# A four-layer graph network on one core: relational values with nodes on partitions, and attention terms spread over partitions by DMA through DRAM

## The chip, the cores and the metric

The kernel runs on one core of a Trainium2 chip. Times are device microseconds (us), the median of several executions. All executions told of here are in the same, fast state. The engines are named as in the profile: PE is TensorE (PEld its weight loads), DVE is VectorE, ACT is ScalarE, POOL is GpSimd, SP is SyncE, which issues most DMAs.

## The reference, cut to what matters

128 graphs of 64 nodes with 256 features each go through four layers, each with a layernorm ahead of it and a residual addition behind it:

```python
h = relu(layernorm(x)); x = x + gat4(h, adj)        # layer 0: attention, 4 heads
h = relu(layernorm(x)); x = x + gat1(h, adj)        # layer 1: attention, 1 head
h = relu(layernorm(x)); x = x + relational(h, adj)  # layer 2
h = relu(layernorm(x)); x = x + ggnn(h, adj)        # layer 3: 3 rounds of A h, then a GRU cell

# attention: e[i,j] = leaky_relu(e_src[i] + e_dst[j], 0.2), softmax over neighbours j,
#            out = elu(softmax @ Wh)
# relational, the part that these 0/1 edges use:
#            v = (h W.T + b) * sigmoid(h W.T Wg.T + bg);  out = relu((adj == 1).T @ v)
```

Everything is float32. The kernel factors the exponential of the leaky ReLU: up to a factor that the softmax cancels, it is max(exp(e_dst), exp(0.2 e_dst) * exp(-0.8 e_src)). The last factor, here called the spread term, belongs to node i, and for the product it must stand along the free axis, the same on all 64 partitions of the graph.

## The kernel before

16 groups of 8 graphs go through a pipeline of four stages, so a steady step has layer 0 of one group, layer 1 of the group before it, the relational layer of the third and the recurrence of the fourth. Their instructions are emitted side by side and ordered by the compiler. The parts that matter:

```python
# attention (both layers): the spread term, by a product with a matrix of ones per graph
nc.gpsimd.tensor_tensor(dg..., diag..., es[:, :, :heads]..., ALU.mult)       # e_src on a diagonal
for c in range(0, gh, step):
    nc.tensor.matmul(pe[:, : n * N], same, dg[:, c : c + n, :]..., ...)
    nc.scalar.activation(t[:, c : c + n, :]..., pe[:, : n * N], AF.Exp, scale=ALPHA - 1.0)
nc.vector.tensor_tensor(t, t, flat(gd), ALU.mult)
nc.vector.tensor_tensor(t, t, flat(fd), ALU.max)
for half in range(2):
    nc.vector.tensor_tensor(eb[b, :, b]..., t[b]..., mt[b]..., ALU.min)      # mask
# ... eb is the stationary operand of the aggregation

def elu_add(work, src, o):                       # end of both attention layers
    nc.vector.tensor_scalar(em, o, 0.0, None, op0=ALU.min)
    nc.scalar.activation(em, em, AF.Exp)
    nc.vector.scalar_tensor_tensor(em, em, -1.0, o, op0=ALU.add, op1=ALU.max)
    nc.gpsimd.tensor_tensor(src, src, em, ALU.add)      # the residual addition, xg<-xg,em

# relational layer: features on partitions, then eight transposes back
for c in range(K):
    for part in range(2):
        for k in range(K):
            nc.tensor.matmul(pm, wl[:, k, col : col + P], hT[:, k, :], ...)
    nc.scalar.activation(sg, pgh[1], AF.Tanh, bias=bl[:, 1, c : c + 1], scale=0.5)
    nc.scalar.activation(vT[:, c, :], pgh[0], AF.Identity, bias=bl[:, 0, c : c + 1])
    nc.vector.scalar_tensor_tensor(vT[:, c, :], sg, 1.0, vT[:, c, :], op0=ALU.add, op1=ALU.mult)
# ... then 4 x 2 nc.tensor.transpose(pt..., vT..., ident), and nc.scalar.copy(v..., pt)

def along(psum, hnat, abd, aT, c):               # recurrence: neighbours' sum
    # four products into pa
    nc.vector.tensor_copy(aT[:, c, :], pa)       # aT feeds the next gate products
```

The waits of TensorE are named below by what it waits for. "hn" is the layernorm's output, which is transposed. "hT" of the recurrence is the new state, which is transposed back (VectorE's last instruction of an update). "aT" is the copied neighbours' sum. "eb" is the masked attention terms, and "hnat" the copy of the recurrence's state with nodes on partitions. VectorE writes all.

Of the kernel before, what the change touches and what calls it, by code (L numbers as in the profile page):

```python
# [8 lines left out]
F32 = mybir.dt.float32  # L9
I32 = mybir.dt.int32  # L10
AF = mybir.ActivationFunctionType
ALU = mybir.AluOpType
# [3 lines left out]
P = 128  # L16
N = 64
D = 256
K = D // P
G = 4  # L20
T = G * P
# [3 lines left out]
ALPHA = 0.2  # L25
# [13 lines left out]
def over_partitions(ap, n):  # L39

    return bass.AP(tensor=ap.tensor, offset=ap.offset, ap=[[0, P], [1, n]])
# [25 lines left out]
def kernel(  # L67
# [28 lines left out]
    nc = tc.nc  # L96
# [14 lines left out]
    ident = const.tile([P, P], F32, name="ident")  # L111
    mhalf = const.tile([P, G], F32, name="mhalf")

    same = const.tile([P, P], F32, name="same")
    diag = const.tile([P, N], F32, name="diag")
# [246 lines left out]
    with ExitStack() as s1:  # L362
        once = s1.enter_context(tc.tile_pool(name="once", bufs=1))
        work = s1.enter_context(tc.tile_pool(name="work", bufs=2))
        psum = s1.enter_context(tc.tile_pool(name="psum", bufs=2, space=PSUM))

        class Layer:


# [7 lines left out]
                    return work.tile(shape, dtype, name=name, tag=name, bufs=self.shared[name])  # L377
                return self.pool.tile(shape, dtype, name=f"{name}{self.layer}", bufs=self.bufs.get(name, 1))

        W = [Layer(0, work, {"wh": 2, "es": 2, "fd": 2, "gd": 2}), Layer(1, work, {}), Layer(2, work, {"sg": 2})]  # L380

        nc.scalar.dma_start(w0e[:, :, :D], rows(W0))
        AT, XG, AG = [], [], []
# [20 lines left out]
        for s in range(2):  # L404
            h = slice(s * N, (s + 1) * N)
# [27 lines left out]
        OH = blocks("oh", G)  # L433
        ABD = blocks("abd", G)
        wl = once.tile([P, K, 2 * D], F32, name="wl")
        bl = once.tile([P, 2, K], F32, name="bl")

        def edge_bounds(g):

# [16 lines left out]
        def attention(g, layer, heads, we, mt):  # L456


            pool = W[layer]
            gh = G * heads  # L460
            src = XG[g]
            wv, es = yield from values(pool, psum, src, heads, we)
            fd = pool.tile([P, G, heads], F32, name="fd")
            gd = pool.tile([P, G, heads], F32, name="gd")
            nc.scalar.activation(fd, es[:, :, heads:], AF.Exp)
            nc.scalar.activation(gd, es[:, :, heads:], AF.Exp, scale=ALPHA)
            dg = pool.tile([P, gh, N], F32, name="dg")
            nc.gpsimd.tensor_tensor(
                dg.rearrange("p (g h) i -> p g h i", g=G),
                diag[:, None, None, :].to_broadcast([P, G, heads, N]),  # L470
                es[:, :, :heads, None].to_broadcast([P, G, heads, N]),
                ALU.mult,
            )
            yield 0.3
            t = pool.tile([P, gh, N], F32, name="t")
            step = 512 // N
            for c in range(0, gh, step):
                n = min(step, gh - c)
                pe = psum.tile([P, 512], F32, name="mm")
                nc.tensor.matmul(  # L480
                    pe[:, : n * N], same, dg[:, c : c + n, :].rearrange("p c i -> p (c i)"), start=True, stop=True
                )
                nc.scalar.activation(
                    t[:, c : c + n, :].rearrange("p c i -> p (c i)"), pe[:, : n * N], AF.Exp, scale=ALPHA - 1.0
                )
                yield 0.86
            flat = lambda d: d.rearrange("p g h -> p (g h)")[:, :, None].to_broadcast([P, gh, N])
            nc.vector.tensor_tensor(t, t, flat(gd), ALU.mult)  # L488
            nc.vector.tensor_tensor(t, t, flat(fd), ALU.max)  # L489
            eb = EB[layer][g % len(EB[layer])]  # L490
            for half in range(2):
                b = slice(half * N, (half + 1) * N)
                nc.vector.tensor_tensor(  # L493
                    eb[b, :, b].rearrange("p (g h) i -> p g h i", g=G),
                    t[b].rearrange("p (g h) i -> p g h i", g=G),
                    mt[b, :, None, :].to_broadcast([N, G, heads, N]),
                    ALU.min,
                )
            yield 0.3
            o = yield from aggregate(pool, psum, lambda p, h: eb[:, p * heads + h, :], wv, heads)  # L500
            elu_add(pool, src, o)

        def later_weights(prep):
            relational_weights(prep, psum, wl, W_loop, Wg_loop, 0.5)
            ihn = prep.tile([P, 6, D], F32, name="ihn")
            nc.scalar.dma_start(ihn, rows(w_ih))
            ihT = prep.tile([P, K, 3 * D], F32, name="ihT")
            transpose_blocks(psum, ihT, ihn, 6)
            hhn = prep.tile([P, 6, D], F32, name="ihn")
            nc.scalar.dma_start(hhn, rows(w_hh))  # L510
            transpose_blocks(psum, whh[:, :, : 2 * D], hhn[:, :4], 4)
            transpose_blocks(psum, whh[:, :, 2 * D :], hhn[:, 4:], 2, 0.5)
            for i in range(LAYERS):
                wn = prep.tile([P, K, D], F32, name="wn")
                nc.scalar.dma_start(wn, rows(weight[i]))
                wT = prep.tile([P, K, D], F32, name="gT")
                transpose_blocks(psum, wT, wn, K)

                for f in range(K):
                    for c0, c1 in ((0, 512), (512, 3 * D)):  # L520
                        pm = psum.tile([P, 512], F32, name="mm")
                        for k in range(K):
                            nc.tensor.matmul(
                                pm[:, : c1 - c0], wT[:, k, f * P : (f + 1) * P], ihT[:, k, c0:c1],
                                start=(k == 0), stop=(k == K - 1),
                            )
                        nc.vector.tensor_copy(wc[:, i, f, c0:c1], pm[:, : c1 - c0])
            with nc.allow_non_contiguous_dma(reason="biases onto partitions"):
                nc.scalar.dma_start(bl[:, 0, :], b_loop.rearrange("o (c p) -> p (o c)", p=P))
                nc.scalar.dma_start(bl[:, 1, :], bg_loop.rearrange("o (c p) -> p (o c)", p=P))  # L530
                nc.scalar.dma_start(bi, b_ih.rearrange("(c p) -> p c", p=P))
                nc.scalar.dma_start(bh, b_hh.rearrange("(c p) -> p c", p=P))
            nc.vector.tensor_scalar(bl, bl, 0.5, None, op0=ALU.mult)
            nc.vector.tensor_tensor(brz, bi[:, :4], bh[:, :4], ALU.add)
            nc.vector.tensor_scalar(brz, brz, 0.5, None, op0=ALU.mult)
            nc.vector.tensor_scalar(bh[:, 4:], bh[:, 4:], 0.5, None, op0=ALU.mult)

        def loop_relation(g):

            pool = W[2]  # L540
            src = XG[g]
            hT = pool.tile([P, K, T], F32, name="hT")
            yield from layernorm_T(pool, psum, src, hT)
            oh = OH[g % 2]
            block_diagonal(oh, AG[g], 1.0, ALU.is_equal)

            vT = pool.tile([P, K, T], F32, name="vT")
            for c in range(K):
                pgh = []
                for part in range(2):  # L550
                    pm = psum.tile([P, T], F32, name="mm")
                    col = part * D + c * P
                    for k in range(K):
                        nc.tensor.matmul(pm, wl[:, k, col : col + P], hT[:, k, :], start=(k == 0), stop=(k == K - 1))  # L554
                    pgh.append(pm)
                    yield 1.72
                sg = pool.tile([P, T], F32, name="sg")
                nc.scalar.activation(sg, pgh[1], AF.Tanh, bias=bl[:, 1, c : c + 1], scale=0.5)
                nc.scalar.activation(vT[:, c, :], pgh[0], AF.Identity, bias=bl[:, 0, c : c + 1])
                nc.vector.scalar_tensor_tensor(vT[:, c, :], sg, 1.0, vT[:, c, :], op0=ALU.add, op1=ALU.mult)  # L560
            v = pool.tile([P, G, D], F32, name="v")
            for q in range(G // 2):
                pt = psum.tile([P, 2, D], F32, name="tp")
                po = psum.tile([P, 2, D], F32, name="mm")
                ps = slice(2 * q, 2 * q + 2)
                for i in range(2):
                    p = 2 * q + i
                    for c in range(K):
                        nc.tensor.transpose(pt[:, i, c * P : (c + 1) * P], vT[:, c, p * P : (p + 1) * P], ident)
                nc.scalar.copy(v[:, ps, :], pt)  # L570
                yield 0.45
                for i in range(2):
                    p = 2 * q + i
                    nc.tensor.matmul(po[:, i, :], oh[:, p, :], v[:, p, :], start=True, stop=True)
                nc.vector.scalar_tensor_tensor(src[:, ps, :], po, 0.0, src[:, ps, :], op0=ALU.max, op1=ALU.add)
                yield 0.86
# [267 lines left out]
```

## Time and profile before

| what | before |
|---|---|
| time, median of 3 runs | 1795.34 us (1793.3 to 1802.8) |
| TensorE busy | 92% |
| VectorE busy | 55% |
| a steady step | 103.4 to 105.9 us |
| TensorE's waits at a step's end | 1.2 us (hT) and 3.3 us (hn) |

The prediction shows the busy shares, the chain, the steps and the step's end. One more view: VectorE in the middle of a step, in time (start, duration, engine, line, operation, output and inputs, shapes, and in brackets its idle time before with what ended it):

```profile
870.92 1.90 DVE L488 TENSOR_TENSOR t<-t,gd 128x1024 f32<-128x1024 f32 x1 [1.48 <-ACT t L483]
872.86 1.22 DVE L489 TENSOR_TENSOR t<-t,fd 128x1024 f32<-128x1024 f32 x1
874.60 0.68 DVE L246 COPY aT<-tp 128x512 f32<-128x512 f32 x1
875.20 2.44 DVE L493 TENSOR_TENSOR eb<-t,mt 64x1024 f32<-64x1024 f32 x2
```

The spread terms t start a block in which VectorE has no idle time, and the copy of aT stands within that block. So its place in the block decides when TensorE gets it.

### The profile page before, as it was taken

To read this page: it belongs to the slowest core of one execution; us is meant where nothing else is said; L and a number is where in the kernel's file an instruction comes from. 1 tells how busy PE (TensorE), PEld (TensorE's weight loads), DVE (VectorE), ACT (ScalarE), POOL (GpSimd) and SP (SyncE) were. 2 spreads that over 40 slices of the span, in tenths; PEclk is the share of its full clock that TensorE was granted. 3 is DMA by queue.
4 is the path that set the end of the run, shared out by engine and by line. 5 is a ranking of instruction groups with operands and counts; after the bars stand their busy time and mean duration, and the time that the engine had idled before them with its cause. 6 is when DMAs were issued, how large, how long until landed. Compare 5 with 4: busy or idle time off the path is not lost.

```text
span 1803.7 us, 16268 instructions
## 1 busy us (share of the span) xinstructions
PE 1660.7 (92%) x5865; PEld 942.7 (52%) x5865; DVE 988.1 (55%) x2269; ACT 510.1 (28%) x897; POOL 312.9 (17%) x269
## 2 busy tenths in 40 slices
PE   3848899999999999999999999999999999999997
PEld 2635555555555555555555555555555555454543
DVE  6555466472746647383665738466573736544433
ACT  1112323223232323323232332333233232222221
POOL 2111212121111212121121212112121211211110
PEclk9868999999999999999999999999999999999998
DMA  5000000010000001000000100000000000000000
GB/s 157 21 3 3 1 4 27 1 29 1 4 27 3 27 0 30 0 12 19 4 27 1 30 1 8 19 4 24 0 27 0 13 0 1 12 1 12 1 12 14
DMA packets 40810, 26.05 MB, mean 14 GB/s; under 512 B 20496, under 2 KB 40720, under 8 KB 40720
## 3 DMA queue, kind: packets, MB, share of 16 engines
q1 hardware_dynamic: 34560, 20.98, 4.1%
q10 hardware_dynamic: 6160, 3.94, 0.8%
q8 instruction: 48, 0.79, 0.2%
q14 instruction: 42, 0.34, 0.1%
HBM read 16.52 MB, written 8.39 MB: 14 GB/s over the span
## 4 chain that ended last, share of the span: by engine, by line
PE 70%; DVE 21%; ACT 3%; POOL 2%; DMA 2%; issue 1%; SPq 0%; ACTq 0%; DVEq 0%; POOLq 0%
PE rz L272 27%; PE nn L272 14%; PE mm L554 6%; PE mm L212 6%; PE mm L229 5%; PE tp L242 4%; PE tp L149 4%; DVE st L132 4%; DVE eb L493 2%; DVE d L306 2%; DVE t L488 2%; PE tp L283 2%; DVE t L489 1%; DVE m L447 1%; DVE em L191 1%
## 5 line engine op out<-in xcount | busy, mean ns | idle before, releaser
L272 PE MATMUL rz<-aT,wc 128*128 128x512 f32 x768 | 398.5, 611 | 0.3 <-DVE aT L246 0.3
L272 PE MATMUL rz<-hT,whh 128*128 128x512 f32 x768 | 386.3, 595 | 0.5 <-ACT hT L150 0.5
L302 POOL TENSOR_TENSOR d<-hT,nt 128x512 f32<-128x512 f32 x96 | 121.5, 1266 | 652.4 <-ACT nt L300 650.9
L272 PEld LDWEIGHTS rz<-aT,wc 128*128 128x128 f32 x768 | 139.9, 193 | 152.7 <-issue 126.6
L272 PEld LDWEIGHTS rz<-hT,whh 128*128 128x128 f32 x768 | 139.6, 191 | 115.3 <-issue 110.0
L272 PE MATMUL nn<-aT,wc 128*128 128x512 f32 x384 | 190.2, 597 | 0.0
L272 PE MATMUL nn<-hT,whh 128*128 128x512 f32 x384 | 189.3, 595 | 0.0
L306 DVE SCALAR_TENSOR_TENSOR d<-z,d 128x512 f32<-128x512 f32 x96 | 86.4, 900 | 160.6 <-POOL d L302 110.6
L149 PE MATMUL tp<-ident,hn 128*128 128x128 f32 x512 | 89.6, 322 | 72.6 <-DVE hn L141 72.5
L296 ACT ACTIVATE t<-nn,bh 128x512 f32<-128x512 f32 x96 | 65.9, 687 | 270.2 <-PE nn L272 270.2
L149 PEld LDWEIGHTS tp<-ident,hn 128*128 128x128 f32 x512 | 73.6, 167 | 122.8 <-issue 67.9
L554 PE MATMUL mm<-hT,wl 128*128 128x512 f32 x256 | 124.6, 600 | 0.0
L229 PEld LDWEIGHTS mm<-wh,eb 128*128 128x128 f32 x640 | 98.4, 213 | 47.6 <-issue 38.7
L137 POOL TENSOR_TENSOR rstd<-var,mhalf 128x4 f32<-128x4 f32 x64 | 66.9, 1045 | 320.7 <-DVE mv L133 165.0
L294 ACT ACTIVATE r<-rz,brz 128x512 f32<-128x512 f32 x96 | 65.9, 686 | 199.9 <-PE rz L272 199.8
L242 PEld LDWEIGHTS tp<-abd,hnat 128*128 128x128 f32 x768 | 99.9, 194 | 42.9 <-issue 22.1
L229 PE MATMUL mm<-wh,eb 128*128 128x65 f32 (+1 forms) x640 | 112.0, 317 | 11.0 <-DVE eb L493 10.2
L272 PEld LDWEIGHTS nn<-hT,whh 128*128 128x128 f32 x384 | 71.8, 191 | 78.2 <-issue 77.5
L217 DVE COPY es<-mm 128x8 f32<-128x8 f32 (+1 forms) x128 | 20.4, 159 | 167.6 <-ACT wh L216 167.6
L297 DVE SCALAR_TENSOR_TENSOR t<-r,t 128x512 f32<-128x512 f32 x96 | 65.9, 687 | 78.0 <-ACT r L294 50.5
L242 PE MATMUL tp<-abd,hnat 128*128 128x128 f32 x768 | 104.6, 280 | 4.1 <-DVE hnat L285 4.1
L246 DVE COPY aT<-tp 128x512 f32<-128x512 f32 x96 | 66.1, 688 | 77.0 <-PE tp L242 77.0
(108 smaller groups left out, 2020.1 us busy)
## 6 DMA issues: line engine op xcount, KB each, us to landing
xg<-in_x_dram SPq DMA_DIRECT2D x16, 512.0 KB, 5.1
out_dram<-hnat SPq DMA_DIRECT2D x16, 512.0 KB, 3.2
at<-in_adj_dram SPq DMA_DIRECT2D x64, 32.0 KB, 3.0
ag<-in_adj_dram SPq DMA_DIRECT2D x16, 128.0 KB, 2.2
ihn<-in_L_gnn_w_ih_dram ACTq DMA_DIRECT2D x1, 768.0 KB, 8.5
ihn<-in_L_gnn_w_hh_dram ACTq DMA_DIRECT2D x1, 768.0 KB, 4.7
wn<-in_L_gnn_weight_dram ACTq DMA_DIRECT2D x3, 256.0 KB, 2.6
w0e<-in_L_gnn_W_dram ACTq DMA_DIRECT2D x1, 256.0 KB, 3.1
```

The source lines that it names most:

```text
L132: nc.vector.bn_stats(st[:, p, :], src[:, p, :])
L137: nc.gpsimd.tensor_tensor(rstd, var, mhalf, ALU.pow)
L149: nc.tensor.transpose(pt[:, p * P : (p + 1) * P], hn[:, p, k * P : (k + 1) * P], ident)
L212: nc.tensor.matmul(pm[:, : D + 2 * heads], hT[:, k, p * P : (p + 1) * P], we[:, k, :], start=(k == 0), stop=(k == K - 1),)
L229: nc.tensor.matmul(pv[:, h, :], lhsT(p, h), wv[:, p, h, :], start=True, stop=True)
L242: nc.tensor.matmul(pa[:, p * P : (p + 1) * P], hnat[:, p, c * P : (c + 1) * P], abd[:, p, :], start=True, stop=True,)
L246: nc.vector.tensor_copy(aT[:, c, :], pa)
L272: nc.tensor.matmul(self.pg, w[:, k, self.chunk * P : (self.chunk + 1) * P], m[:, k, :], start=(self.done == 0), stop=(self.done == self.n ...
L294: nc.scalar.activation(r, pr, AF.Tanh, bias=brz[:, c : c + 1], scale=0.5)
L302: nc.gpsimd.tensor_tensor(d, hT[:, c, :], nt, ALU.subtract)
L306: nc.vector.scalar_tensor_tensor(d, z, 1.0, d, op0=ALU.add, op1=ALU.mult)
L554: nc.tensor.matmul(pm, wl[:, k, col : col + P], hT[:, k, :], start=(k == 0), stop=(k == K - 1))
```

## The change

The intent is to take work off TensorE, which is busy 92% of the time. The relational values are computed with nodes on partitions (the operands of the product swapped), so the eight transposes go. The bias then lies along the free axis and VectorE adds it. The spread terms are exponentiated while small, transposed, written as one row to DRAM, and read back to 64 partitions twice. That replaces a GpSimd product, TensorE products with "same" and large exponentials, from the fourth group on.

```diff
# attention, for g >= 3 (groups 0 to 2 keep the product)
-            nc.gpsimd.tensor_tensor(dg..., diag..., es..., ALU.mult)
-            ... nc.tensor.matmul(pe[:, : n * N], same, dg..., ...)
-                nc.scalar.activation(t..., pe..., AF.Exp, scale=ALPHA - 1.0)
+                fs = pool.tile([P, G, heads], F32, name="fs")
+                nc.scalar.activation(fs, es[:, :, :heads], AF.Exp, scale=ALPHA - 1.0)
+                nc.tensor.transpose(pt[:gh, :P], fs.rearrange("p g h -> p (g h)"), ident)
+                nc.vector.tensor_copy(fT, pt[:gh, :P])
+                row = dram.tile([2, gh * N], F32, name=f"row{layer}")
+                nc.sync.dma_start(row..., fT...)
+                for half in range(2):
+                    nc.sync.dma_start(
+                        t[half * N : (half + 1) * N].rearrange("p c i -> p (c i)"),
+                        row[half : half + 1, :].to_broadcast([N, gh * N]),
+                    )
# relational layer
-            ... products to features on partitions, 2 Tanh, 2 Identity with bias, 8 transposes, copies
+            for p in range(G):
+                for k in range(K):
+                    nc.tensor.matmul(pm, hT[:, k, p * P : (p + 1) * P], wl[:, k, :], ...)
+                nc.vector.tensor_tensor(u, pm, bl, ALU.add)
+                nc.scalar.activation(u[:, D:], u[:, D:], AF.Tanh, scale=0.5)
+                nc.vector.scalar_tensor_tensor(v[:, p, :], u[:, D:], 1.0, u[:, :D], op0=ALU.add, op1=ALU.mult)
```

More of the change, by code (lines that the diff above doesn't have):

```diff
@@ L365 @@
         psum = s1.enter_context(tc.tile_pool(name="psum", bufs=2, space=PSUM))
+        dram = s1.enter_context(tc.tile_pool(name="dram", bufs=2, space=bass.MemoryType.DRAM))
         class Layer:
@@ L378, in tile @@
                 return self.pool.tile(shape, dtype, name=f"{name}{self.layer}", bufs=self.bufs.get(name, 1))
-        W = [Layer(0, work, {"wh": 2, "es": 2, "fd": 2, "gd": 2}), Layer(1, work, {}), Layer(2, work, {"sg": 2})]
+        W = [Layer(0, work, {"wh": 2, "es": 2, "fd": 2, "gd": 2}), Layer(1, work, {}), Layer(2, work, {"u": 2})]
         nc.scalar.dma_start(w0e[:, :, :D], rows(W0))
@@ L435 @@
         wl = once.tile([P, K, 2 * D], F32, name="wl")
-        bl = once.tile([P, 2, K], F32, name="bl")
+        bl = once.tile([P, 2 * D], F32, name="bl")
         def edge_bounds(g):
@@ L466, in attention @@
             nc.scalar.activation(gd, es[:, :, heads:], AF.Exp, scale=ALPHA)
-            dg = pool.tile([P, gh, N], F32, name="dg")
-            nc.gpsimd.tensor_tensor(
-                dg.rearrange("p (g h) i -> p g h i", g=G),
-                diag[:, None, None, :].to_broadcast([P, G, heads, N]),
-                es[:, :, :heads, None].to_broadcast([P, G, heads, N]),
-                ALU.mult,
-            )
-            yield 0.3
-            t = pool.tile([P, gh, N], F32, name="t")
-            step = 512 // N
@@ L477, in attention @@
-            for c in range(0, gh, step):
-                n = min(step, gh - c)
-                pe = psum.tile([P, 512], F32, name="mm")
-                nc.tensor.matmul(
-                    pe[:, : n * N], same, dg[:, c : c + n, :].rearrange("p c i -> p (c i)"), start=True, stop=True
-                )
-                nc.scalar.activation(
-                    t[:, c : c + n, :].rearrange("p c i -> p (c i)"), pe[:, : n * N], AF.Exp, scale=ALPHA - 1.0
-                )
-                yield 0.86
+            t = pool.tile([P, gh, N], F32, name="t")
@@ new lines, in attention @@
+            if g < 3:
+                dg = pool.tile([P, gh, N], F32, name="dg")
+                nc.gpsimd.tensor_tensor(
+                    dg.rearrange("p (g h) i -> p g h i", g=G),
+                    diag[:, None, None, :].to_broadcast([P, G, heads, N]),
+                    es[:, :, :heads, None].to_broadcast([P, G, heads, N]),
+                    ALU.mult,
+                )
+                yield 0.3
+                step = 512 // N
+                for c in range(0, gh, step):
+                    n = min(step, gh - c)
+                    pe = psum.tile([P, 512], F32, name="mm")
+                    nc.tensor.matmul(
+                        pe[:, : n * N], same, dg[:, c : c + n, :].rearrange("p c i -> p (c i)"), start=True, stop=True
+                    )
+                    nc.scalar.activation(
+                        t[:, c : c + n, :].rearrange("p c i -> p (c i)"), pe[:, : n * N], AF.Exp, scale=ALPHA - 1.0
+                    )
+                    yield 0.86
+            else:
+                fs = pool.tile([P, G, heads], F32, name="fs")
+                nc.scalar.activation(fs, es[:, :, :heads], AF.Exp, scale=ALPHA - 1.0)
+                pt = psum.tile([P, T], F32, name="tp")
+                nc.tensor.transpose(pt[:gh, :P], fs.rearrange("p g h -> p (g h)"), ident)
+                fT = pool.tile([gh, P], F32, name="fT")
+                nc.vector.tensor_copy(fT, pt[:gh, :P])
+                yield 0.3
+                row = dram.tile([2, gh * N], F32, name=f"row{layer}")
+                nc.sync.dma_start(row.rearrange("a (c i) -> c a i", i=N), fT.rearrange("c (a i) -> c a i", i=N))
+                for half in range(2):
+                    nc.sync.dma_start(
+                        t[half * N : (half + 1) * N].rearrange("p c i -> p (c i)"),
+                        row[half : half + 1, :].to_broadcast([N, gh * N]),
+                    )
+                yield 1.3
@@ L527, in later_weights @@
                         nc.vector.tensor_copy(wc[:, i, f, c0:c1], pm[:, : c1 - c0])
+            for i, b in enumerate((b_loop, bg_loop)):
+                nc.sync.dma_start(bl[:, i * D : (i + 1) * D], over_partitions(b[0:1], D))
             with nc.allow_non_contiguous_dma(reason="biases onto partitions"):
-                nc.scalar.dma_start(bl[:, 0, :], b_loop.rearrange("o (c p) -> p (o c)", p=P))
-                nc.scalar.dma_start(bl[:, 1, :], bg_loop.rearrange("o (c p) -> p (o c)", p=P))
                 nc.scalar.dma_start(bi, b_ih.rearrange("(c p) -> p c", p=P))
                 nc.scalar.dma_start(bh, b_hh.rearrange("(c p) -> p c", p=P))
-            nc.vector.tensor_scalar(bl, bl, 0.5, None, op0=ALU.mult)
+            nc.vector.tensor_scalar(bl[:, :D], bl[:, :D], 0.5, None, op0=ALU.mult)
             nc.vector.tensor_tensor(brz, bi[:, :4], bh[:, :4], ALU.add)
@@ L545, in loop_relation @@
             block_diagonal(oh, AG[g], 1.0, ALU.is_equal)
-            vT = pool.tile([P, K, T], F32, name="vT")
-            for c in range(K):
-                pgh = []
-                for part in range(2):
-                    pm = psum.tile([P, T], F32, name="mm")
-                    col = part * D + c * P
-                    for k in range(K):
-                        nc.tensor.matmul(pm, wl[:, k, col : col + P], hT[:, k, :], start=(k == 0), stop=(k == K - 1))
-                    pgh.append(pm)
-                    yield 1.72
-                sg = pool.tile([P, T], F32, name="sg")
-                nc.scalar.activation(sg, pgh[1], AF.Tanh, bias=bl[:, 1, c : c + 1], scale=0.5)
-                nc.scalar.activation(vT[:, c, :], pgh[0], AF.Identity, bias=bl[:, 0, c : c + 1])
-                nc.vector.scalar_tensor_tensor(vT[:, c, :], sg, 1.0, vT[:, c, :], op0=ALU.add, op1=ALU.mult)
-            v = pool.tile([P, G, D], F32, name="v")
+            v = pool.tile([P, G, D], F32, name="v")
+            for p in range(G):
+                pm = psum.tile([P, 2 * D], F32, name="mm")
+                for k in range(K):
+                    nc.tensor.matmul(pm, hT[:, k, p * P : (p + 1) * P], wl[:, k, :], start=(k == 0), stop=(k == K - 1))
+                u = pool.tile([P, 2 * D], F32, name="u")
+                nc.vector.tensor_tensor(u, pm, bl, ALU.add)
+                nc.scalar.activation(u[:, D:], u[:, D:], AF.Tanh, scale=0.5)
+                nc.vector.scalar_tensor_tensor(v[:, p, :], u[:, D:], 1.0, u[:, :D], op0=ALU.add, op1=ALU.mult)
+                yield 1.72
             for q in range(G // 2):
-                pt = psum.tile([P, 2, D], F32, name="tp")
                 po = psum.tile([P, 2, D], F32, name="mm")
                 ps = slice(2 * q, 2 * q + 2)
-                for i in range(2):
-                    p = 2 * q + i
-                    for c in range(K):
-                        nc.tensor.transpose(pt[:, i, c * P : (c + 1) * P], vT[:, c, p * P : (p + 1) * P], ident)
-                nc.scalar.copy(v[:, ps, :], pt)
-                yield 0.45
                 for i in range(2):
```

## The prediction

> **What bounds the kernel now.** I read the page's busy shares and its chain of waits first, then the windows of six whole group steps (the 16 groups go through a four-stage pipeline, so the steady part repeats one step), then the order in time of TensorE, VectorE and GpSimd around a step's end and its middle.
>
> ```profile
> PE 1660.7 (92%) x5865; PEld 942.7 (52%) x5865; DVE 988.1 (55%) x2269; ACT 510.1 (28%) x897; POOL 312.9 (17%) x269
> PE 70%; DVE 21%; ACT 3%; POOL 2%; DMA 2%; issue 1%; SPq 0%; ACTq 0%; DVEq 0%; POOLq 0%
> ```
>
> TensorE is the bound: 92% busy and 70% of the chain. But VectorE holds 21% of that chain, so TensorE does not run free. The windows of single steps (length, busy time of PE, PEld, DVE, ACT and POOL, granted clock, DMA) show how much it loses:
>
> ```profile
> 491.90:595.30 103.40, 98.95 (x361) 55.86 (x360) 60.65 (x139) 31.55 (x56) 19.25 (x17) 1.00 0.05 13
> 595.30:700.39 105.09, 100.64 (x361) 56.93 (x360) 60.66 (x138) 31.77 (x56) 19.27 (x17) 0.98 0.05 13
> 1013.98:1119.93 105.95, 101.50 (x361) 57.81 (x361) 60.83 (x140) 31.77 (x56) 19.26 (x17) 0.97 0.04 13
> ```
>
> A step is 103.4 us when the clock stays at 1.00 and 1.7 to 2.5 us longer when part of it ran at half clock. The losses sit at the step's end (TensorE and VectorE in time):
>
> ```profile
> 803.13 2.35 POOL L192 TENSOR_TENSOR xg<-xg,em 128x1024 f32<-128x1024 f32 x1 [1.80 <-DVE em L191]
> 803.80 2.22 DVE L306 SCALAR_TENSOR_TENSOR d<-z,d 128x512 f32<-128x512 f32 x1 [0.75 <-ACT z L305]
> 807.38 0.63 PE L283 MATMUL tp<-ident,hT 128*128 128x128 f32 x4 [1.03 <-DVE hT L307]
> 813.21 1.02 PE L272 MATMUL nn<-aT,wc 128*128 128x512 f32 x2
> 817.46 1.82 PE L149 MATMUL tp<-ident,hn 128*128 128x128 f32 x8 [3.23 <-DVE hn L141]
> ```
>
> TensorE waits 1.2 us for the last state (start to start, against its usual 0.43 us per pass), then 3.4 us for the next groups' layernorm. That is 4.6 us in each step, plus about 2 us of half clock behind it.
>
> **What the Trainium skill says.** "TensorE: Matmul & The Clock Gate", Part 1 (the HAM clock gate): a window of about 3.4 us without enough work puts the array at half clock for at least one more window. The trace agrees: after the 3.4 us wait, the eight transposes at 817.46 take 1.62 us start to start, those at 823.01 take 0.87. "GPSIMD Engine Reference", Specifications: GpSimd shares its SBUF interfaces with VectorE, and instructions with two SBUF inputs or in a two-port mode contend. The trace agrees: the update at 803.80 took 2.22 us and ended only after GpSimd's addition; elsewhere it takes 0.69. "DMA: Bandwidth & Descriptors", Anatomy of one DMA: about 2.0 us fixed plus bytes at 436 GB/s. The trace agrees for the 128 KB of edges (2.2 us), not for the broadcast of a 1 KB vector to 128 partitions, also 128 KB (4.5 us):
>
> ```profile
> ag<-in_adj_dram SPq DMA_DIRECT2D x16, 128.0 KB, 2.2
> ab<-in_L_gnn_a_dram ACTq DMA_DIRECT2D x2, 128.0 KB, 4.5
> ```
>
> **The change, part by part.** TensorE's cost is read from starts, as ends are modelled. Mid-step:
>
> ```profile
> 868.56 0.60 PE L569 MATMUL tp<-ident,vT 128*128 128x128 f32 x4
> 869.00 1.02 PE L480 MATMUL mm<-dg,same 128*128 128x512 f32 x2
> 869.86 1.88 PE L272 MATMUL rz<-hT,whh 128*128 128x512 f32 x4
> 875.05 0.59 PE L480 MATMUL mm<-dg,same 128*128 128x256 f32 x2
> 875.48 1.02 PE L272 MATMUL rz<-hT,whh 128*128 128x512 f32 x2
> ```
>
> Four transposes take 0.44 us, a 512-column fp32 product 0.86 (two passes), a 256-column one 0.43.
> - Relational part, all 16 groups: the value product stays at eight 512-column fp32 products. Eight transposes go: 2 x 0.44 = 0.87 us of TensorE.
> - Attention, from group 3 on (13 groups): two 512-column and one 256-column product with "same" go: 2 x 0.86 + 0.43 = 2.15 us. Two small transposes come: 2 x 0.11 = 0.22.
> - Net TensorE per full step: 0.87 + 2.15 - 0.22 = 2.8 us, 2.7% of 105.1.
> - ScalarE: the value part goes from 2 x 0.69 + 2 x 0.69 + 2 x 0.59 = 3.9 us to 4 x 0.38 = 1.5 us; three exponentials (2 x 0.59 + 0.38) become two of 0.2. It loses 3.5 us, at 28% busy, off the path.
> - GpSimd: the two spread products (1.90 + 0.63 us) go.
> - VectorE: two of 0.69 us become four bias additions from PSUM at 0.69 and four half-width products at 0.42, so 1.4 us becomes 4.4; two copies of 0.15 come. That is +3.3 us per step, 60.7 to 64. It has room on average, not everywhere: in before it has no gap from 870.9 to 885.7 us.
> - DMA: per group 8 KB to DRAM, then 2 x 256 KB to 64 partitions each; 2 KB and 2 x 64 KB for layer 1. The first is wanted in a chain: transpose, copy, write, two reads, then VectorE.
>
> If all of the TensorE time came off: 13 x 2.8 + 3 x 0.87 = 39 us, 1756. I don't expect all of it, because the scheduler has moved other things, and the stalls are part of the step. I laid out the compiled order of the changed kernel by hand over the stalls, each instruction with its duration from the trace.
>
> Step's end. In the changed order the first residual addition on GpSimd (2.35 us) falls between two VectorE instructions: VectorE's next layernorm statistics wait for it, and the update of the state stands behind them in the queue. The 2.22 us contention goes, this wait comes. From the first transposes back (900.04 in before) to the first layernorm transposes, before takes 22.5 us with 17.9 of products. After, I get 21.5 to 22.0 us with 16.15 of products: some of the products have left that stretch. So the waits there become 5.4 to 5.9 instead of 4.6 us, again in two pieces, with the half clock as before.
>
> Step's middle, time 0 at the small transpose of layer 0. VectorE reaches the first multiplication of the spread terms at about 8.0 us. Its DMAs should be there: copy to 0.5, write 2.2, two issues, reads 3.1 to 5.1 (those for 256 KB of weights and for 512 KB of x), so 6.3 to 8.3. From there VectorE has no gap to about 20.4. TensorE wants the layernorm transposes at 21.8 and gets them at about 22.3 (0.5 us), and wants the next product with aT at 26.0, which VectorE gives at 27.6 (up to 1.6 us, less if the first multiplication, no longer beside GpSimd's subtraction, takes 1.22 instead of 1.9). I take 1.0 us in all.
>
> Sum for a full step: -2.8 (TensorE) + 1.0 (waits at the end) + 1.0 minus the 0.5 there was (middle) = -1.3 us. Over 13 steps -17 us, and -2.5 us for the transposes in three other steps: **1776 us**, 1.1% less.
>
> **Rivals.**
> - The TensorE time comes off whole (1756), or the end's waits also fall under a clock window and the half clock's 2 us go as well (1756 - 26 = 1730). For it: 92% busy, 70% of the chain, and the contention of 2.22 us is gone. Against it: the waits are VectorE's chain, which the change lengthens.
> - The DMA becomes the wait. For it: the 1 KB broadcast took 4.5 us, 2.3 more than the same bytes read from different places, some 50 GB/s over the fixed part. At that rate 512 KB need 10 us more, VectorE stands 7 us or so in each step with TensorE behind it, and the half clock follows: 13 x (7 - 1.3), about 1870. Against it: each read is 4 KB from an 8 KB row, not 1 KB, and x's 512 KB land in 5.1 us. I give the full form one chance in twenty, a milder one (1 to 2 us a step, 1785 to 1800) one in four.
> - VectorE becomes the bound of the middle entirely (the 1.6 us in full, waits of 5.9 at the end): -2.8 + 1.3 + 1.6 = +0.1 per step, unchanged at 1794.
>
> **Range and chances.** The centre is the sum above; one microsecond of error per step is 13 us, and both stretches have about that, on either side. So 1745 to 1806. Faster by over 2% means under 1759, which needs the first rival: 0.24. Slower by over 2% (over 1831) needs the DMA in full: 0.06. Within 2%: 0.70.
>
> **What would show it.** The removed work: no transposes of vT, no products with "same" after the third group, TensorE's busy time down by some 30 us and VectorE's up by some 45. The end: GpSimd's addition as the releaser of VectorE's statistics, the wait for hT near 2 us and for hn near 3.4, and PEclk still dipping to about 0.98 in most steps. The middle: a wait of TensorE for hn or aT there, 0.5 to 2 us; VectorE's wait for the DMA of t under 1 us. I am wrong if the reads of the row land over 5 us after issue, if hT or hn are waited for less than in before, or if steps come out under 102 us.

## The result, and the profile after

The changed kernel is correct and takes 1774.87 us (median of 4 runs, 1769.41 to 1777.7) beside 1796.45 us for the kernel before (4 runs, 1793.3 to 1802.8). The ratio is 0.9872, with a 95% interval of 0.9833 to 0.991: 1.3% faster, within 2%. Ratios here are the mean time of one kernel's fast runs over that of the other's in the same rounds, so they are not quite the ratio of the quoted medians.

The page of the kernel after, busy shares and chain:

```profile
PE 1622.8 (91%) x5685; PEld 916.2 (52%) x5685; DVE 1019.6 (57%) x2391; ACT 459.8 (26%) x852; POOL 294.6 (17%) x243
PE 63%; DVE 23%; issue 6%; POOL 6%; DMA 2%; ACT 1%; SPq 0%; ACTq 0%; POOLq 0%; DVEq 0%
```

TensorE lost 38 us of busy time, but the span only 28 (1803.7 to 1775.3 in the two profiled runs). TensorE's share of the chain fell from 70% to 63%; the chain now runs more through VectorE and GpSimd. DMA stays at 2% although HBM reads rose from 16.5 to 25.3 MB.

Three whole steps of the kernel after (start:end, length, then busy time of PE, PEld, DVE, ACT and POOL, granted clock, DMA share, GB/s):

```profile
590.34:694.86 104.52, 98.95 (x349) 56.04 (x348) 62.39 (x147) 28.46 (x54) 17.86 (x14) 0.97 0.07 20
798.33:901.28 102.95, 97.37 (x349) 55.04 (x348) 62.38 (x147) 28.34 (x54) 17.86 (x14) 0.98 0.07 20
901.28:1003.23 101.95, 96.39 (x349) 54.18 (x348) 62.31 (x147) 28.24 (x54) 17.86 (x14) 1.00 0.07 20
```

A step has 12 matrix instructions less (349, not 361), and it is 1.4 us or more shorter than before at the same granted clock (104.52 beside 105.95 at 0.97, 101.95 beside 103.40 at 1.00). On average over nine steps it is only 1.1 us shorter, as the clock stays whole in one of them and not in three. Its step's end, in time:

```profile
791.58 2.35 POOL L192 TENSOR_TENSOR xg<-xg,em 128x1024 f32<-128x1024 f32 x1
793.97 0.75 DVE L132 BATCH_NORM_STATS2 st<-xg 128x6 f32<-128x256 f32 x2 [3.47 <-POOL wh L207]
794.85 0.66 DVE L306 SCALAR_TENSOR_TENSOR d<-z,d 128x512 f32<-128x512 f32 x1
796.50 0.66 PE L283 MATMUL tp<-ident,hT 128*128 128x128 f32 x4 [1.56 <-DVE hT L307]
799.53 2.46 POOL L192 TENSOR_TENSOR xg<-xg,em 128x1024 f32<-128x1024 f32 x1 [5.56 <-DVE em L191]
799.70 2.32 DVE L136 TENSOR_SCALAR var<-mv 128x4 f32<-128x4 f32 x1
806.35 2.21 PE L149 MATMUL tp<-ident,hn 128*128 128x128 f32 x8 [2.97 <-DVE hn L141]
```

VectorE stands 3.47 us behind GpSimd's first addition (a short memset behind it in GpSimd's queue has the last semaphore). The update L306 itself is back to 0.66 us from 2.22. But four elements per partition (L136) now take 2.32 us, because GpSimd's second addition runs: that starts 0.17 us earlier, and both end at 802.0. The contention has only moved. The Trainium skill's "SBUF — State Buffer", section "SBUF: two separate sides", calls the pair of ports that VectorE and GpSimd share an exclusive lock, held for the whole instruction, on which the loser blocks. The equal ends here agree with it, as does the kernel before, where L306 ended 0.54 us (less than its own 0.69) after the addition.

The step's middle:

```profile
849.12 0.28 DVE L498 COPY fT<-tp 16x128 f32<-16x128 f32 x1
856.79 1.22 DVE L509 TENSOR_TENSOR t<-t,gd 128x1024 f32<-128x1024 f32 x1
859.50 1.97 POOL L302 TENSOR_TENSOR d<-hT,nt 128x512 f32<-128x512 f32 x1 [8.51 <-ACT nt L300]
860.46 2.09 DVE L514 TENSOR_TENSOR eb<-t,mt 64x1024 f32<-64x1024 f32 x1
864.52 1.08 PE L229 MATMUL mm<-wh,eb 128*128 128x65 f32 x8 [0.24 <-DVE eb L514]
875.90 0.69 DVE L246 COPY aT<-tp 128x512 f32<-128x512 f32 x1
876.65 1.13 PE L272 MATMUL rz<-aT,wc 128*128 128x512 f32 x2 [0.80 <-DVE aT L246]
```

VectorE starts the first multiplication of the spread terms at 856.79 without an idle bracket: the transfer is there before it is wanted. The rates of the DMA from 849 to 857 us say how long before, in 40 slices of 0.2 us each:

```profile
GB/s 0 0 0 0 0 0 40 1 0 0 0 0 0 0 0 164 246 328 348 184 164 266 184 328 246 164 0 0 0 0 0 0 0 0 0 0 0 0 0 0
```

The 8 KB row goes out at 850.2 and the 512 KB come back between 852.0 and 854.4, 2.4 us ahead of VectorE. What TensorE does wait for is VectorE: 0.24 us for eb and 0.80 for aT in the brackets, which is 0.40 and 0.96 against the usual interval from start to start.

The contention has moved here too. Before, GpSimd's subtraction (L302) stretched VectorE's first multiplication to 1.90 us; now that takes 1.22, but the first mask product (L514) falls beside the subtraction and takes 2.09 us, where it took 1.21 before. VectorE's queue has no idle time from 856.79 to 869.3, so these 0.9 us delay all that stands behind.

My own sums over nine steady steps of each trace (third to twelfth output store) say where the step's time goes. "Work" is TensorE's instructions at their usual start-to-start interval (the lower quartile for each kind); a wait is the excess over that interval where the trace records idle time, by what ended it; "rest" is the remainder: instructions at half clock, and about 1 us that is there at full clock too (e4, e5). All in us per step:

```
                                step    work    hT    hn    aT    eb   hnat   rest
before                        104.71   97.35  1.19  3.34              0.35   2.48
after                         103.59   94.54  1.73  3.22  0.96  0.40         2.74
e1 relational part only       105.05   96.47  1.00  3.40              1.07   3.11
e2 spread by DMA only         105.63   95.42  1.93  3.72  0.53  0.73         3.30
e4 after, residual on VectorE  98.40   94.55  0.36  1.02  0.96  0.40         1.11
e5 before, residual on VectorE 99.86   97.35        1.07              0.35   1.09
```

TensorE's work fell by 2.81 us a step, the waits and the rest took 1.7 back, and 1.1 was left.

### The profile page after: what moved, and what is told of

Same layout as the page of the kernel before. It is cut to its first block, busy times and chain, and to the rows that moved or that the text cites. A ratio compares the mean times of both kernels' runs of the same rounds, so it can differ in the third digit from the quotient of the medians.

```text
span 1775.3 us, 16054 instructions
## 1 busy us (share of the span) xinstructions
PE 1622.8 (91%) x5685; PEld 916.2 (52%) x5685; DVE 1019.6 (57%) x2391; ACT 459.8 (26%) x852; POOL 294.6 (17%) x243
## 4 chain that ended last, share of the span: by engine, by line
PE 63%; DVE 23%; issue 6%; POOL 6%; DMA 2%; ACT 1%; SPq 0%; ACTq 0%; POOLq 0%; DVEq 0%
PE rz L272 24%; PE nn L272 12%; PE mm L571 6%; PE mm L212 6%; PE tp L149 4%; DVE st L132 4%; PE mm L229 3%; PE tp L242 3%; DVE eb L514 3%; POOL xg L192 2%; POOL rstd L137 2%; DVE var L136 2%; PE tp L283 2%; DVE hn L141 1%; POOL d L302 1%
## 5 line engine op out<-in xcount | busy, mean ns | idle before, releaser
L272 PE MATMUL rz<-aT,wc 128*128 128x512 f32 x768 | 391.5, 602 | 8.9 <-DVE aT L246 8.9
L302 POOL TENSOR_TENSOR d<-hT,nt 128x512 f32<-128x512 f32 x96 | 136.0, 1417 | 939.9 <-ACT nt L300 939.9
L272 PE MATMUL nn<-aT,wc 128*128 128x512 f32 x384 | 197.1, 616 | 0.0
L150 ACT ACTIVATE hT<-tp 128x512 f32<-128x512 f32 x128 | 71.7, 595 | 235.6 <-PE tp L149 230.1
L132 DVE BATCH_NORM_STATS2 st<-xg 128x6 f32<-128x256 f32 x256 | 97.2, 405 | 50.4 <-POOL wh L207 41.6
L571 PE MATMUL mm<-wl,hT 128*128 128x512 f32 x256 | 124.3, 599 | 0.0
L229 PEld LDWEIGHTS mm<-wh,eb 128*128 128x128 f32 x640 | 94.8, 213 | 54.3 <-issue 52.0
L306 DVE SCALAR_TENSOR_TENSOR d<-z,d 128x512 f32<-128x512 f32 x96 | 67.7, 705 | 85.6 <-ACT z L305 43.2
L141 DVE TENSOR_SCALAR hn<-xg,mv,rstd 128x256 f32<-128x256 f32 x256 | 88.0, 411 | 38.7 <-POOL rstd L137 33.7
```

What stands on the lines that cost most here:

```text
L132: nc.vector.bn_stats(st[:, p, :], src[:, p, :])
L141: nc.vector.tensor_scalar(hn[:, p, :], src[:, p, :], mv[:, p, 0:1], rstd[:, p : p + 1], op0=ALU.subtract, op1=ALU.mult,)
L150: nc.scalar.activation(hT[:, k, :], pt, AF.Relu)
L229: nc.tensor.matmul(pv[:, h, :], lhsT(p, h), wv[:, p, h, :], start=True, stop=True)
L272: nc.tensor.matmul(self.pg, w[:, k, self.chunk * P : (self.chunk + 1) * P], m[:, k, :], start=(self.done == 0), stop=(self.done == self.n ...
L302: nc.gpsimd.tensor_tensor(d, hT[:, c, :], nt, ALU.subtract)
```

## The experiments

Eleven kernels ran, in three batches, each batch on one chip with runs of the kernel before between them: 1801.74 us in the first batch (11 runs), 1801.01 in the second and 1800.63 in the third (9 each). All but e3 and e10 are correct.

### e1 and e2: each part alone

e1 keeps the relational part and the product for all groups; e2 keeps the relational layer of before and spreads by DMA.

```diff
# e1, in the changed kernel
-            if g < 3:
+            if g < 16:
# e2: the changed kernel with loop_relation and its biases as before
```

> The relational part alone; the attention terms are spread by the product in all groups. Theory A (TensorE's gain is given back by VectorE's 3 us of added work in the middle of the step): TensorE loses 0.87 us per step, a wait for aT or hn of 0.5 to 1 us comes, so 1788 to 1798 us, within 0.5% of before. Theory B (removed TensorE time comes off whole): 16 x 0.87 = 14 us less, 1782.

> The attention part alone; the relational values keep their transposes. Theory A: VectorE has no added work beyond two copies of 0.28 us, so TensorE's 1.93 us per step come off nearly whole over 13 steps: 25 us, about 1771 (1765 to 1778), as fast as the whole change. Theory C (the DMA through DRAM costs a wait): over 1785, with VectorE waiting for t.

e1 took 1793.46 us (ratio 0.9962, 0.9941 to 0.9983), within theory A's range, but not by A's waits: aT isn't waited for and hn hardly more (3.40 us, before 3.34); what grew is the wait for hnat (0.35 to 1.07). e2 took 1801.77 us (ratio 1.0003, 0.9982 to 1.0025): theory A's 1771 is missed by 31 us, although TensorE lost 1.93 us of work in each step, as worked out. Theory C's wait for the transfer isn't the reason either. The middle of a step of e2:

```profile
870.67 1.22 DVE L509 TENSOR_TENSOR t<-t,gd 128x1024 f32<-128x1024 f32 x1
873.74 2.09 DVE L514 TENSOR_TENSOR eb<-t,mt 64x1024 f32<-64x1024 f32 x1
878.31 1.10 PE L229 MATMUL mm<-wh,eb 128*128 128x65 f32 x8 [0.57 <-DVE eb L514]
```

L509 has no idle time before it. The mask product L514 is stretched beside GpSimd as in the changed kernel. By the sums above, more waiting for hT (+0.74), hn (+0.38), eb (+0.73) and aT (+0.53) and a longer rest (+0.82) ate the 1.93 us and more, and only the wait for hnat (-0.35) went; what the steady steps lost so, the pipeline's first and last steps gave back. Each of these waits is released by VectorE, and yet VectorE has less to do in e2 than before (59.0 us busy a step on average, not 60.6). So the amount of its work alone doesn't decide. The two parts are not additive: 8 us and 0 us alone, some 22 together.

### e3: VectorE's four bias additions taken away

```diff
-                nc.vector.tensor_tensor(u, pm, bl, ALU.add)
-                nc.scalar.activation(u[:, D:], u[:, D:], AF.Tanh, scale=0.5)
+                nc.scalar.activation(u[:, D:], pm[:, D:], AF.Tanh, scale=0.5)   # and pm[:, :D] in the product
```

> The changed kernel without VectorE's four bias additions (wrong on purpose: the relational biases are left out; tanh and the product read PSUM). VectorE has 2.4 us less per step. Theory A: the 1.0 us wait for aT in the middle and the 0.2 us for eb go, 13 x 1.2 = 15 us, so about 1760 (1752 to 1766). Theory B (the middle wait is set by something else, such as the layernorm's GpSimd step): 1771 to 1777.

The result is wrong (relative error 0.049). It took 1776.46 us (ratio 0.9864, 0.9841 to 0.9887), the same as the changed kernel, and hT, hn and aT are waited for 1.73, 3.22 and 0.96 us as there. Theory A falls and B holds: 2.8 us less of VectorE's work in each step are worth nothing where they lie in its idle gaps.

### e4: the residual addition on VectorE

```diff
 def elu_add(work, src, o):
-        nc.gpsimd.tensor_tensor(src, src, em, ALU.add)
+        nc.vector.tensor_tensor(src, src, em, ALU.add)
```

> The changed kernel with the residual addition after each attention layer on VectorE (1.2 us) in place of GpSimd (2.35 us). Theory D (the end of the step is lost to GpSimd's addition, which VectorE waits 3.5 us for, and to the starving of VectorE's two-port instructions beside it): the 1.7 us wait for hT goes, that for hn falls from 3.1 to about 2.3, part of the half clock goes: 2.5 to 4 us per step, about 1730 (1715 to 1745). Theory E (VectorE is the bound and 2.4 us more work there costs as much): 1775 to 1800.

1698.31 us (ratio 0.9432, 0.941 to 0.9455). Theory D had the mechanism right, but the gain is beyond its range: 5.2 us a step, where it said 2.5 to 4. A step's end in e4:

```profile
753.74 1.69 POOL L302 TENSOR_TENSOR d<-hT,nt 128x512 f32<-128x512 f32 x1 [3.45 <-ACT nt L300]
754.34 2.17 DVE L192 TENSOR_TENSOR xg<-xg,em 128x1024 f32<-128x1024 f32 x1
757.29 0.67 DVE L306 SCALAR_TENSOR_TENSOR d<-z,d 128x512 f32<-128x512 f32 x1
758.95 0.66 PE L283 MATMUL tp<-ident,hT 128*128 128x128 f32 x4 [0.20 <-DVE hT L307]
767.60 1.53 PE L149 MATMUL tp<-ident,hn 128*128 128x128 f32 x8 [0.91 <-DVE hn L141]
```

VectorE does the addition in 1.2 us when GpSimd doesn't read beside it (here 2.17), against 2.35 on GpSimd, and no longer stands between. The wait for hT nearly goes (1.73 to 0.36 us), that for hn fell from 3.2 to 1.0 us, and with waits this short the clock stays whole:

```profile
662.50:760.90 98.40, 96.25 (x349) 54.13 (x348) 62.83 (x149) 28.12 (x53) 13.04 (x12) 1.00 0.07 21
```

The waits for hT and hn and the rest fell by 5.2 us together, the whole gain of a step; aT and eb are waited for as before. This shows what the step's end costs in the changed kernel (e5 does the same for the kernel before): GpSimd's addition in VectorE's chain, and the half clock behind the waits.

### e5 to e7: the same edit in the kernel before and in the two halves of the change

Was the end's wait also what ate the change's gain? Then, without it, the change should be worth its TensorE time.

```diff
# e5: before, e6: e1, e7: e2, each with
-        nc.gpsimd.tensor_tensor(src, src, em, ALU.add)
+        nc.vector.tensor_tensor(src, src, em, ALU.add)
```

> The kernel before, with only the residual addition moved from GpSimd to VectorE. Theory F (the waits at the step's end, made by GpSimd's addition, swallowed what the change takes off TensorE; with them gone TensorE's time counts whole): a step is TensorE's work of 97.4 us plus 2.5 to 3.5 of waits and half clock, about 100.5, and the whole is 39 us above the changed kernel with the same edit (1698): 1730 to 1740. Theory G (the change is worth its 22 us whatever the end of the step does): 1720.

> Relational part alone, residual addition on VectorE. Theory F: 14 us under the kernel before with the same edit, so 1716 to 1726. Theory G (as measured without the edit): 7 us under it.

> Attention part alone, residual addition on VectorE. Theory F: 25 us under the kernel before with the same edit, so 1705 to 1715. Theory G (as measured without the edit: nothing): equal to it.

| | time, us | ratio (95%) | under e5 |
|---|---|---|---|
| e5, before | 1724.72 | 0.9574 (0.9552 to 0.9596) | |
| e6, relational part | 1716.08 | 0.9533 (0.9512 to 0.9554) | 8.6 |
| e7, spread by DMA | 1716.05 | 0.9539 (0.9518 to 0.956) | 8.7 |
| e4, both | 1698.31 | 0.9432 (0.941 to 0.9455) | 26.4 |

e4 ran in the batch before, where the kernel before took nearly the same time (1801.74 and 1801.01). e5 lies halfway between theory G's 1720 and F's 1730 to 1740. e6 is near G's 7 us, and e7 lies between F's 25 and G's 0. So neither theory holds whole. Without GpSimd's addition the change is worth 26 us, hardly more than the 22 with it, of 39 us of TensorE's time. The end's wait is a large loss of both kernels, but it explains little of what the change didn't bring. In e6 a wait of 1.07 us for hnat remains, in e7 0.74 for eb and 0.53 for aT, in e4 0.96 for aT and 0.40 for eb, each in the middle and each released by VectorE.

The comparison of e5 and e4 also shows where the gain does arrive. Their profiled spans differ by 26.5 us, and TensorE's work by 40:

| stretch | TensorE's work, e5 to e4 | time, e5 to e4 |
|---|---|---|
| to the third output store | -11.5 | -10.1 |
| nine steady steps | -25.2 | -13.1 |
| from the twelfth store | -3.6 | -3.2 |

Outside the steady steps, where fewer stages run side by side, the work comes off nearly whole. In the steady steps half of it does.

### e8: the copy of aT moved to ScalarE as well

```diff
# e4 and, in along()
-        nc.vector.tensor_copy(aT[:, c, :], pa)
+        nc.scalar.copy(aT[:, c, :], pa)
```

> The changed kernel with the residual addition on VectorE and the copy of aT out of PSUM on ScalarE in place of VectorE. Theory H (the 0.96 us wait for aT in the middle of each step is VectorE's queue: the copy stands behind statistics and masks): it goes, 13 x 1 us, and so do short ones: 1680 to 1690. Theory I (it moves to another instruction of the same queue): 1695 to 1702.

1688.27 us (ratio 0.9374, 0.9355 to 0.9394), in theory H's range. The wait for aT is gone, and the step fell from 98.40 to 97.56 us. That is 0.1 less than aT's 0.96: the wait for eb grew from 0.40 to 0.66 us, while the rest fell a little. This version is the fastest that ran, and beats both kernels.

### e9: each spread read twice

If the transfers are hidden, doubling their bytes should cost nothing.

```diff
-                for half in range(2):
+                for half in (0, 1, 0, 1):
                     nc.sync.dma_start(t[half * N : (half + 1) * N]..., row[half : half + 1, :]...)
```

> The changed kernel, with each spread read from DRAM issued twice (the second writes the same bytes over the first), so that the spread terms' transfers take at least 2.3 us more and two more issues. Theory J (the transfers are hidden with some 2 us to spare, and the compiler's order puts more VectorE work ahead of the first multiplication when it sees the longer chain): between 1770 and 1790 us, VectorE stands no microsecond before the first multiplication of layer 0's terms. Theory K (the transfers are at the edge of the path): VectorE and then TensorE stand 2 to 4 us more in each of 13 steps, 1800 to 1830 us.

1762.72 us (ratio 0.9789, 0.9772 to 0.9807): not slower than the changed kernel but 12 us faster (15 by the ratios; the two ran in different batches), below theory J's range, and theory K is refuted. The middle of a step of e9:

```profile
853.84 1.28 DVE L509 TENSOR_TENSOR t<-t,gd 128x1024 f32<-128x1024 f32 x1
855.25 0.67 DVE L246 COPY aT<-tp 128x512 f32<-128x512 f32 x1
855.85 1.20 DVE L510 TENSOR_TENSOR t<-t,fd 128x1024 f32<-128x1024 f32 x1
857.14 2.42 DVE L514 TENSOR_TENSOR eb<-t,mt 64x1024 f32<-64x1024 f32 x2
862.88 0.42 DVE L509 TENSOR_TENSOR t<-t,gd 128x256 f32<-128x256 f32 x1 [0.20 <-DMA t<-row]
```

The 1 MB of packets ran from 845.97 to 852.54, and VectorE still starts layer 0's terms without idle time, 1.3 us later; only layer 1's show waiting, 0.2 us in this step. Since the chain is longer, the compiler put more of VectorE's work ahead of the first multiplication, and now places a copy of aT between the multiplication and the maximum. TensorE's waits for aT and eb are gone (0.96 and 0.40 to 0), hT and hn are as in the changed kernel (1.72, 3.29), TensorE's work is unchanged (94.55), and the step is 102.45 us, 1.1 less. So with the same arithmetic, another compiled order is worth what the change gained per step. It isn't the order of VectorE's queue alone: GpSimd's subtraction no longer falls beside the mask products either, which take 2.42 us for both, where the changed kernel needs 3.31, and TensorE's products are ordered differently as well. No run separates these.

### e10: the maximum over the spread terms left out

```diff
# e4 and
-            nc.vector.tensor_tensor(t, t, flat(fd), ALU.max)
```

> The changed kernel with the residual addition on VectorE, and without the maximum over the attention terms: wrong on purpose, 1.2 us less for VectorE in layer 0 and some 0.4 us in layer 1 in each step, TensorE's work the same. Theory L (what is left of the loss is VectorE's queue in the step's middle): the wait for aT (0.96 us a step) goes, as may part of the wait for hn (1.02), so the step falls from 98.4 to between 96.5 and 97.6 us, 1675 to 1690 us in all. Theory M (the middle's wait has another cause, such as the transfer or ScalarE): aT is waited for as before, 1695 to 1700 us.

The result is wrong (relative error 0.082). It took 1691.48 us (ratio 0.9396, 0.9378 to 0.9413), a step 97.76 us: just above theory L's ranges, under M's. The waits for aT and eb go, as L says, and 0.67 us for hnat comes, which it doesn't say. 1.6 us less in VectorE's block made the step 0.6 us shorter.

### e11: the first three groups by DMA as well

```diff
# e8 and
-            if g < 3:
+            if g < 0:
```

> The best version so far (residual on VectorE, copy of aT on ScalarE), with the attention terms of the first three groups also spread by the transfers instead of the product. Theory N (in the first steps TensorE waits for other things, and the chain through DRAM is exposed there): 0 to 10 us slower, 1688 to 1698 us. Theory O (the product costs TensorE there what it costs later): 3 groups x 2.15 us less, about 1682 us.

1688.94 us (ratio 0.938, 0.9365 to 0.9395), the same as e8 (0.7 us apart, with ranges of 1 to 3). Theory N's lower edge holds, O's 1682 doesn't. TensorE's products of those groups cost nothing on balance; why (the start waits for other things, or the exposed chain gives it back) was not taken apart.

## Why the prediction was right or wrong

The predicted 1776 us and the measured 1774.87 agree, and so does the difference within the run's own round: -19.5 predicted (-17 and -2.5), -21.6 measured.

- **TensorE's work, -2.8 us a step: right.** The start-to-start sums give -2.81. Its busy time fell by 38 us, where I had written some 30.
- **The waits at the step's end, 5.4 to 5.9 instead of 4.6: mechanism right, size too large.** GpSimd's addition did fall between two instructions of VectorE, which then waited 3.47 us for it, and the clock went on dipping. But hT and hn together rose from 4.53 to 4.95 us, so by 0.4 and not by 0.8 to 1.3. Of the two, only hT rose (1.19 to 1.73); hn fell from 3.34 to 3.22, against the statement that it would not: by the letter a sign of being wrong, by 0.12 us. I counted on L306 losing its contention, but not on L136 catching it (2.32 us).
- **The middle, 1.0 instead of 0.5: right in kind.** aT is waited for 0.96 us ("up to 1.6"), and eb for 0.40, which I hadn't named; the layernorm's 0.5 did not come as a wait of its own. Together 1.36 us, where hnat's 0.35 went: +1.0, not +0.5, about as much too small as the end was too large. The first multiplication did shorten to 1.22 us, as I had allowed for; that the mask product would be stretched in its place (to 2.09) I had not.
- **Hidden DMA: right, with more slack than I gave it.** I put its landing 6.3 to 8.3 us after the small transpose, with VectorE at 8.0. It landed 5.6 us after it, 2.4 us ahead of VectorE, and e9 doubled the bytes with no loss. The rival with a milder form of the DMA wait, at one in four, was given too much. What it rested on was misread. The 1 KB broadcast's 4.5 us were taken in the crowded start of the kernel (issued at 15.8 and 21.3 us), where two loads of 128 KB of edges took 5.2 us to land, not 2.2 as in the median of all 16. So they show no cost of a broadcast.
- **VectorE's work, +3.3 us a step, 60.7 to 64: mis-sized.** It is 62.4, and over the whole run 31.5 us more, not 45. Four additions at 0.69 us are as worked out, the narrow products took 0.47 and the copies of fT 0.28, so more; but L306 (900 to 705 ns on average) and the first multiplication (1777 to 1218 ns) shortened, as no GpSimd instruction reads beside them any more. The wide mask products (1215 to 1567 ns) and L136 lengthened, as one now does. And "which the change lengthens" was the wrong reason: e3 took 2.8 us of this away and gained nothing, and e2 lost 1.6 us of VectorE's work and waited more. What counts is what stands in its queue in the two stretches, in which order, and beside which of GpSimd's instructions.
- **The sum, -1.3 over 13 full steps and -2.5 in the others: right in total, mis-divided, so that it agrees to 2 us is partly luck.** The nine steady steps gave -1.1 each, 10 us. The rest came from the steps in which the pipeline fills and drains. I had put four of them into the 13, with waits that they don't have, so 8 us for filling and draining. In the traces of the two kernels these stretches are 18 us shorter for 14 us of work (the traces differ by 28 us, the medians by 22, as the traced execution of the kernel before was a long one); with the residual on VectorE, where the clock disturbs less, 13 us for 15.
- **A step under 102 us:** one of nine came out at 101.95, at a granted clock of 1.00. That is a sign of being wrong by its letter, by 0.05 us. Its waits are those of the other steps, only the clock stayed whole, and on average the steps take 103.6, so the statement's point stands.

What stays open is why the two parts alone gain so much less than together. The waits that come differ with each compiled order (hnat in e1; eb and aT in e2; aT in the changed kernel), and e9 shows that another order of the same arithmetic can be worth 12 us. TensorE waits for eb or aT only in runs in which a wide mask product is stretched to some 2 us beside GpSimd's subtraction, and in none of those in which both take 1.2 (before, e1, e5, e6, e9). That points to the contention, but doesn't prove it: before, e1, e5 and e6 have the first multiplication stretched in its place (1.6 to 1.9 us). No run moved the subtraction off GpSimd, or held the order fixed while it changed the work.

## What to carry to other kernels

Work taken off the busiest engine comes off the time only where that engine isn't waiting for another's queue: add up its start-to-start intervals, and read the rest of the step as waits by releaser. Before moving work, look for an instruction of a slower engine in the middle of another engine's chain; here moving one addition from GpSimd to VectorE was worth three and a half times the whole change (76 us; moving the copy of aT as well gave 10 more). And a change in the program also changes the compiled order of engines that it hardly touches, and with it which of VectorE's and GpSimd's instructions fall beside each other. So try the parts alone, and expect their gains not to add up.

## What the Trainium skill lacked or had wrong

- "DMA: Bandwidth & Descriptors", Anatomy of one DMA: about 2.0 us fixed plus the bytes at 436 GB/s. The second spread read was issued at 851.31 and the packets of both (512 KB) had ended at 854.38, while the row's write, issued at 849.42, let the first read be issued at 850.78: 1.36 us for 8 KB to DRAM, under the page's fixed part. The page fits the formula to DMAs issued by GpSimd, and these are SyncE's, so the prediction used it outside its range; for SyncE's the page gives a first-byte latency but no such fit. It has no figure for a broadcast either: here two reads of a 4 KB row each, to 64 partitions, took 2.3 to 2.8 us of packets for 512 KB together in most groups.
- "TensorE: Matmul & The Clock Gate", Part 1: how much work in a window is enough to keep the full clock has no figure. Here waits of 1.7 and 3.2 us in a step, some 7 us of work apart, brought the mean clock to 0.97 or 0.98 in eight of nine steps; waits of 1 us (e4) left it at 1.00 in all nine. In the kernel before, nearly the same idle times in every step (1.0 and 3.0 to 3.2 us) left it at 1.00 in three of nine and not in six, so the waits alone don't fix the clock.
- No page says what an order imposed by the compiler is worth. Here it was 12 us of 1775 (e9), with the contention that came and went with it.
